# The four sums of each attention head's features, made by GpSimd instead of VectorE

## The chip, the cores and the metric

One Trainium2 chip, one core. The metric is the time of the whole kernel on the device in microseconds, as the median of repeated executions. TensorE (PE) multiplies, VectorE (DVE), ScalarE (ACT) and GpSimd (POOL) do elementwise work, SyncE (SP) issues transfers; POOL issues transfers as well. Each engine works through its own instructions in the order in which they stand in the program. Engines wait for each other through semaphores.

## The reference

32 graphs of 512 nodes. Each goes through a layer norm with ReLU and two graph attention layers (four heads of 256 features, then one head of 512), and the result is added to the input. Cut to what matters here:

```python
def gat_layer(x, mask, W, a_src, a_dst, bias, concat):
    xl = (x @ W).reshape(B, N, H, F)
    asrc = jnp.einsum('bnhf,hf->bnh', xl, a_src)
    adst = jnp.einsum('bnhf,hf->bnh', xl, a_dst)
    e = jax.nn.leaky_relu(asrc[:, :, None, :] + adst[:, None, :, :], 0.2)
    e = jnp.where(mask[..., None], e, -1e9)
    attn = jax.nn.softmax(e, axis=1)
    out = jnp.einsum('bsdh,bshf->bdhf', attn, xl)      # the gather
    ...
h = jnp.maximum(_layernorm(x, axis=-1), 0.0)
h = jax.nn.elu(gat_layer(h, mask, W1, att_src1, att_dst1, b1, concat=True))
x = x + gat_layer(h, mask, W2, att_src2, att_dst2, b2, concat=False)
```

All of it is f32.

## The kernel before

**Products by seven.** The large products are made by a scheme of the Strassen kind: each operand is cut into two by two blocks, sums and differences of blocks are formed, and seven block products take the place of eight. The first gather, attention times features of one head, is one of them. `sums1` (L1277) forms the sums for one head: on the left from the features `xl` (s1 = a21 + a22, s2 = s1 - a11, a21 = a11 - a21, s4 = a12 - s2; 128 x 256 elements each), on the right from the attention `p` (t1, t2 and two more; 128 x 512 each). s1, s2 and s4 are put into `hs`, the third one is written over a block of `xl`. s4 takes the place of s2 and so can only be made when the sixth product has read s2; the third product needs it. For the last graph (`apart`) s4 has a place of its own, `hs4`. `gather1` (L1334) runs the seven products of the heads, two heads at a time (`PAIRS_OF`): 1, 5, 2, 6, 7, 3, 4, each for one head and then for the other. One product is a step of two matmuls on PE, into one of eight PSUM banks (`mm`). Behind it ACT or DVE takes the result out (`h1` in names of the trace is `h`), or, after the first product, ACT copies the bank into a second one in which the second product goes on adding (`mm<-mm`). The bank is free for others after that.

The first gather is made in this way for 31 of the 32 graphs; graph 0 uses plain products (`gather1_plain`). That makes 31 x 4 heads with four sums of features each.

**What runs beside it.** The loop over graphs (L1611) interleaves the first gather of one graph with the projection of the next one (`project1`: `ht` times `w1_sb` (`w_sb` in the trace), with sums of its own in `hs`, `hx` and `wx`, into `xl`), the projection to the second layer (`project2`: `h1` times `w2_sb`, into `xl2`) and the second gather (`gather2`). The attention `p` of a head is made in `second` (L948): DVE adds and takes the maximum, POOL issues two transfers that add the mask to `p` in place (`p<-dm`, `accumulate`, L522), ACT takes the exponential. Then DVE makes the sums of `p`. POOL has besides these transfers one small operation a graph, the power in the norm (L770).

**What sets the order.** The code doesn't issue its work where it stands. `Program.add` records every step with its engine, a cost written out by hand, and what it reads and writes. At the end `order` (L299) runs a list scheduler over all of it: each engine takes, of the steps whose inputs are there by the costs and by a table of latencies between engines (`PAIRS`, `CROSS`), the one with the lowest rank. A rank is a due time out of the long table `PLACES`, repeated for each graph. The transfers of SP and POOL run on modelled queues. The steps are then issued in the order that comes out, and on the chip each engine keeps to it, whether the costs were right or not. So the cost and the engine of a step have a say in the order of all the others. The table of ranks is the same before and after.

Of the kernel before, what the change touches and what calls it, by code (L numbers as in the profile page):

```python
# [378 lines left out]
def tile_gat(  # L379
# [36 lines left out]
    nc = tc.nc  # L416
# [94 lines left out]
    prog = Program()  # L511
# [3 lines left out]

    def dve(cost, reads, writes, f, *a, **k):
        prog.add("DVE", cost, reads, writes, lambda: f(*a, **k))  # L517

    def dma(size, reads, writes, to, at, cost=0.4):
        prog.add("SP", cost, reads, writes, lambda: nc.sync.dma_start(to, at), size)  # L520
# [46 lines left out]
    def sums_of_weights(w_sb, keys, cost):  # L567
        b11, b21, b22, t4, t1, t2, t3 = (w_sb[:, i] for i in range(7))
        sub = nc.vector.tensor_sub
        dve(cost, keys(6) + keys(0), keys(4), sub, t1, t3, b11)  # L570
        dve(cost, keys(2) + keys(4), keys(5), sub, t2, b22, t1)
        dve(cost, keys(2) + keys(6), keys(6), sub, t3, b22, t3)
        dve(cost, keys(1) + keys(5), keys(3), sub, t4, b21, t2)
# [253 lines left out]
    def p_keys(pk, us=range(NT), cs=range(2)):  # L827

        return [pk + (u, c) for u in us for c in cs]
# [447 lines left out]
    def sums1(h, pk, p, apart):  # L1277


        def a_block(i, j):  # L1280
            return (
                xl[:, 2 * j : 2 * j + 2, h, 2 + i * P : 2 + (i + 1) * P],
                [("xl", 2 * j + k, h, i) for k in range(2)],
            )

        def b_block(r, c):
            return (
                p[:, 2 * r : 2 * r + 2, c * M : (c + 1) * M], p_keys(pk, (2 * r, 2 * r + 1), (c,))
            )

        a11, a12, a21, a22 = (a_block(i, j) for i in range(2) for j in range(2))
        b11, b12, b21, b22 = (b_block(r, c) for r in range(2) for c in range(2))
        k = KQ + h % 2
        s1, s2 = (
            (hs[:, i, k, :].rearrange("p (k f) -> p k f", f=P), [("hs", i, k)]) for i in range(2)
        )
        s4 = s2
        if apart:
            s4 = (hs4[:, h % 2, :].rearrange("p (k f) -> p k f", f=P), [("hs", 2, h % 2)])
        t1, t2 = (  # L1300
            (t.rearrange("p (k f) -> p k f", f=M), [q]) for q, t in (ts_.take() for _ in range(2))
        )

        def op(cost, f, to, u, v):
            dve(cost, u[1] + v[1], to[1], f, to[0], u[0], v[0])

        add, sub = nc.vector.tensor_add, nc.vector.tensor_sub
        op(0.34, add, s1, a21, a22)
        op(0.602, sub, t1, b12, b11)
        op(0.34, sub, s2, s1, a11)  # L1310
        op(0.602, sub, t2, b22, t1)
        op(0.34, sub, a21, a11, a21)
        op(0.602, sub, b12, b22, b12)
        if apart:
            op(0.34, sub, s4, a12, s2)
        return (
            {1: a11, 2: a12, 3: s4, 4: a22, 5: s1, 6: s2, 7: a21},
            {1: b11, 2: b21, 3: b22, 4: b21, 5: t1, 6: t2, 7: b12},
            lambda: op(0.602, sub, b21, b21, t2),
            (lambda: None) if apart else (lambda: op(0.34, sub, s4, a12, s2)),  # L1320
        )


# [10 lines left out]
    def gather1(soft, order):  # L1334
# [3 lines left out]
        for h in sorted(ahead):  # L1338
            blocks[h] = sums1(h, *soft.p[h], order is SINGLY)
        for h, n in order:  # L1340
            if h not in blocks:
                blocks[h] = sums1(h, *soft.p[h], order is SINGLY)
# [367 lines left out]
```

## Time and profile before

| what | us |
|---|---|
| median of the runs shown (2766.06 and 2766.17) | 2766.11 |
| span of the profiled execution | 2767.6 |
| granted TensorE clock, mean | 0.999 of full |
| ACT busy | 2229.1 |
| POOL busy with issuing mask transfers (314) | 273.2 |
| DMA engines, mean busy share from 100 to 2600 us | 0.69 |

The span runs from the first to the last instruction of the program in one profiled execution; the median is that of executions timed by themselves. Names: `out<-in` are the program's tiles. L517 records all of DVE's steps, L514 ACT's, L531 PE's, so groups are told apart by tiles. A PE step of two matmuls stands in the trace as four instructions. In the rows of a group stand the busy time, the mean of one in ns, and then the idle time of the engine just before, with what ended it. A row of the timeline has the start, the duration, the engine, and in brackets the idle time before it. A row of waits has the total, the number and the longest.

### The profile page before, as it was taken

To read this page: it belongs to the slowest core of one execution; us is meant where nothing else is said; L and a number is where in the kernel's file an instruction comes from. 1 tells how busy PE (TensorE), PEld (TensorE's weight loads), DVE (VectorE), ACT (ScalarE), POOL (GpSimd) and SP (SyncE) were. 2 spreads that over 40 slices of the span, in tenths; PEclk is the share of its full clock that TensorE was granted. 3 is DMA by queue.
4 is the path that set the end of the run, shared out by engine and by line. 5 is a ranking of instruction groups with operands and counts; after the bars stand their busy time and mean duration, and the time that the engine had idled before them with its cause. 6 is when DMAs were issued, how large, how long until landed. Compare 5 with 4: busy or idle time off the path is not lost. (4 is left out here: it accounts for less than half of the span.)

```text
span 2767.6 us, 42320 instructions
## 1 busy us (share of the span) xinstructions
PE 2742.4 (99%) x12924; PEld 2371.8 (86%) x12924; DVE 2558.2 (92%) x6732; ACT 2229.1 (81%) x4907; POOL 313.1 (11%) x356
## 2 busy tenths in 40 slices
PE   7999999999999999999999999999999999999999
PEld 6788888888888888888888888888888888888887
DVE  8999999999999999999999999999999999999996
ACT  5978888778887788877888877888778788788883
POOL 0110111101111111111011111111111111101110
PEclk9999999999999999999999999999999999999999
DMA  8657766667666667667676766766676767767563
GB/s 232 176 157 182 203 167 184 187 176 194 182 183 179 182 176 196 178 175 195 173 201 172 182 187 178 192 186 180 180 188 175 201 167 180 195 165 208 162 171 112
DMA packets 375864, 502.14 MB, mean 181 GB/s; under 512 B 222804, under 2 KB 227668, under 8 KB 375636
## 3 DMA queue, kind: packets, MB, share of 16 engines
q1 hardware_dynamic: 329844, 332.68, 42.4%
q0 software_dynamic: 45792, 166.74, 25.1%
q8 instruction: 103, 1.69, 0.3%
q14 instruction: 125, 1.02, 0.1%
HBM read 316.41 MB, written 51.31 MB: 133 GB/s over the span
## 5 line engine op out<-in xcount | busy, mean ns | idle before, releaser
L531 PE MATMUL mm<-w_sb,hs 128*128 128x257 f32 (+3 forms) x2908 | 667.0, 367 | 5.1 <-ACT mm L514 3.3
L531 PEld LDWEIGHTS mm<-w_sb,hs 128*128 128x128 f32 x2908 | 539.7, 190 | 87.7 <-ACT mm L514 6.7
L525 POOL DMA_DIRECT2D p<-dm x314 | 273.2, 875 | 2295.0 <-DVE p L517 764.3
L531 PE MATMUL mm<-w_sb,ht 128*128 128x258 f32 x2112 | 528.6, 382 | 2.7 <-ACT mm L514 2.5
L531 PE MATMUL mm<-p,xl 128*128 128x258 f32 (+1 forms) x1984 | 495.8, 383 | 0.1
L531 PE MATMUL mm<-w_sb,h 128*128 128x257 f32 x2056 | 477.8, 379 | 0.0
L517 DVE SCALAR_TENSOR_TENSOR p<-rr,z 128x512 f32<-128x512 f32 (+1 forms) x636 | 456.0, 742 | 2.4 <-DMA rr<-drr 2.4
L531 PEld LDWEIGHTS mm<-w_sb,ht 128*128 128x128 f32 x2112 | 393.7, 190 | 63.6 <-ACT mm L514 6.4
L514 ACT ACTIVATE p<-p,z 128x512 f32<-128x512 f32 (+1 forms) x636 | 433.4, 720 | 17.7 <-DVE p L517 12.4
L531 PEld LDWEIGHTS mm<-w_sb,h 128*128 128x128 f32 x2056 | 389.0, 189 | 58.4 <-ACT xl L514 0.5
L531 PEld LDWEIGHTS mm<-p,xl 128*128 128x128 f32 x1984 | 367.2, 190 | 52.7 <-issue 6.0
L514 ACT ACTIVATE mm<-mm 128x257 f32<-128x257 f32 (+2 forms) x498 | 169.8, 347 | 269.2 <-PE mm L531 236.2
L514 ACT ACTIVATE l<-as,z 128x512 f32<-128x512 f32 x516 | 354.4, 716 | 30.8 <-DMA as<-das 30.7
L514 ACT ACTIVATE l<-l,low 128x512 f32<-128x512 f32 x516 | 370.3, 721 | 7.6 <-DVE low L517 6.7
L517 DVE CUSTOM_DVE_ANT_1 l<-l,mt 128x512 f32<-128x512 f32 x516 | 346.2, 681 | 28.4 <-ACT l L514 27.4
L514 ACT ACTIVATE xl<-mm 128x258 f32<-128x258 f32 (+2 forms) x748 | 269.3, 382 | 91.4 <-PE mm L531 89.8
L514 ACT ACTIVATE h<-mm,b_sb 128x256 f32<-128x256 f32 (+1 forms) x504 | 231.0, 480 | 77.3 <-PE mm L531 76.6
L531 PE MATMUL mm<-t,hs 128*128 128x258 f32 (+1 forms) x992 | 246.1, 380 | 0.0
L517 DVE TENSOR_TENSOR xl<-xl,mm 128x258 f32<-128x258 f32 x372 | 155.3, 419 | 57.9 <-PE mm L531 48.3
L531 PEld LDWEIGHTS mm<-t,hs 128*128 128x128 f32 x992 | 185.8, 190 | 25.5 <-DVE t L517 0.2
L531 PE MATMUL mm<-xl,p 128*128 128x258 f32 (+2 forms) x752 | 189.7, 388 | 1.0 <-ACT h L514 0.6
L517 DVE SCALAR_TENSOR_TENSOR h<-xr,h 128x512 f32<-128x512 f32 x256 | 172.2, 683 | 6.1 <-ACT xr L514 6.1
(137 smaller groups left out, 3706.2 us busy)
## 6 DMA issues: line engine op xcount, KB each, us to landing
p<-dm POOLq DMA_DIRECT2D x314, 512.0 KB, 5.0
rr<-drr SPq DMA_DIRECT2D x159, 512.0 KB
x<-in_x_dram SPq DMA_DIRECT2D x129, 256.0 KB
adj<-in_adj_dram SPq DMA_DIRECT2D x128, 256.0 KB
as<-das SPq DMA_DIRECT2D x64, 512.0 KB
t<-in_x_dram SPq DMA_DIRECT2D x124, 256.0 KB
out_dram<-t SPq DMA_DIRECT2D x124, 256.0 KB
dm<-m SPq DMA_DIRECT2D x64, 256.0 KB
```

Source lines behind the costliest of these rows:

```text
L514: prog.add("ACT", cost, reads, writes, lambda: nc.scalar.activation(*a, **k))
L517: prog.add("DVE", cost, reads, writes, lambda: f(*a, **k))
L525: lambda: nc.gpsimd.dma_start(to, at, accum_op=OP.add), size,
L531: f(*a, **k)
```

## The change

A helper `pool` records steps for POOL, and the four sums of features in `sums1` are recorded through it, with a cost of 0.75 in place of 0.34. The sums of `p` stay on DVE. What is computed is the same.

```diff
+    def pool(cost, reads, writes, f, *a, **k):
+        prog.add("POOL", cost, reads, writes, lambda: f(*a, **k))
+
...
-        add, sub = nc.vector.tensor_add, nc.vector.tensor_sub
-        op(0.34, add, s1, a21, a22)
+        def feature(f, to, u, v):
+            pool(0.75, u[1] + v[1], to[1], f, to[0], u[0], v[0])
+
+        sub = nc.vector.tensor_sub
+        feature(nc.gpsimd.tensor_add, s1, a21, a22)
         op(0.602, sub, t1, b12, b11)
-        op(0.34, sub, s2, s1, a11)
+        feature(nc.gpsimd.tensor_sub, s2, s1, a11)
         op(0.602, sub, t2, b22, t1)
-        op(0.34, sub, a21, a11, a21)
+        feature(nc.gpsimd.tensor_sub, a21, a11, a21)
         op(0.602, sub, b12, b22, b12)
         if apart:
-            op(0.34, sub, s4, a12, s2)
+            feature(nc.gpsimd.tensor_sub, s4, a12, s2)
...
-            (lambda: None) if apart else (lambda: op(0.34, sub, s4, a12, s2)),
+            (lambda: None) if apart else (lambda: feature(nc.gpsimd.tensor_sub, s4, a12, s2)),
```

The lines of the changed kernel are numbered three higher from here on (L534 is PE's). The order of the steps changes on every engine. Three places:

PE, where the fourth product of one head (into bank `mm_136`, from `p_103`) is followed by the first of the next pair (`p_102`, into the same bank), amid steps of the projection (operands `w_sb`, `ht`, `hs`, `hx`, `wx`). Before:

```order
L531 MATMUL mm_136<-p_103,xl 128x256 x2
L531 MATMUL mm_138<-w_sb,hs 128x129
L531 MATMUL mm_137<-wx_85,hx_86 128x129
L531 MATMUL mm_132<-w_sb,ht 128x258 x2
L531 MATMUL mm_137<-w_sb,hs 128x129
L531 MATMUL mm_138<-w_sb,hx_86 128x129
L531 MATMUL mm_136<-p_102,xl 128x258
L531 MATMUL mm_136<-p_102,xl 128x256
L531 MATMUL mm_137<-wx_85,hs 128x129
L531 MATMUL mm_138<-w_sb,hs_84 128x258 x2
L531 MATMUL mm_137<-w_sb,ht 128x258 x2
```

The same place now:

```order
L534 MATMUL mm_132<-w_sb,ht 128x258 x2
L534 MATMUL mm_133<-p_104,xl 128x256 x2
L534 MATMUL mm_139<-w_sb,ht 128x258 x2
L534 MATMUL mm_136<-p_103,xl 128x256 x2
L534 MATMUL mm_136<-p_102,xl 128x258
L534 MATMUL mm_136<-p_102,xl 128x256
L534 MATMUL mm_133<-p_102,xl 128x256 x2
L534 MATMUL mm_132<-w_sb,hs 128x258 x2
```

The first product of the new head now stands directly behind the fourth of the old one, whose bank ACT has to empty in between, and directly behind it stands its second product (`mm_133`), for which ACT has to copy the bank first; before, five rows of the projection stood at the first of these places and five, three of which are shown, at the second.

PE, in the projection of the same graph, with bank `mm_133`. Before:

```order
L531 MATMUL mm_133<-w_sb,hs 128x258 x2
L531 MATMUL mm_135<-w_sb,hs 128x258 x2
L531 MATMUL mm_133<-w_sb,ht 128x258 x2
L531 MATMUL mm_139<-w_sb,hs_84 128x258 x2
L531 MATMUL mm_135<-w_sb,ht 128x258 x2
```

Now:

```order
L534 MATMUL mm_139<-w_sb,hs_84 128x258 x2
L534 MATMUL mm_133<-w_sb,hs 128x258 x2
L534 MATMUL mm_133<-w_sb,ht 128x258 x2
L534 MATMUL mm_135<-w_sb,ht 128x258 x2
L534 MATMUL mm_137<-w_sb,hs_84 128x258 x2
```

The step of `mm_135` that stood between the two steps of `mm_133` has moved away.

POOL, over some half of a graph, with the mask transfers (DMA) of a few heads. Before:

```order
L525 DMA p_103<-dm_122 128x1024 x2
L525 DMA p_104<-dm_121 128x1024 x2
L525 DMA p_102<-dm_121 128x1024 x2
L770 TENSOR_TENSOR stats_123<-stats_123,half 128x4
L525 DMA p_103<-dm_121 128x1024 x2
```

Now:

```order
L528 DMA p_102<-dm_121 128x1024
L520 TENSOR_TENSOR hs<-xl 128x256 x2
L520 TENSOR_TENSOR xl<-xl 128x2x128 x2
L528 DMA p_102<-dm_121 128x1024
L773 TENSOR_TENSOR stats_123<-stats_123,half 128x4
L520 TENSOR_TENSOR hs<-hs,xl 128x256 x2
L520 TENSOR_TENSOR hs<-xl 128x256
L520 TENSOR_TENSOR xl<-xl 128x2x128
L520 TENSOR_TENSOR hs<-xl 128x256
L520 TENSOR_TENSOR xl<-xl 128x2x128
L520 TENSOR_TENSOR hs<-xl,hs 128x256
L528 DMA p_103<-dm_121 128x1024 x2
```

Four sums now stand between the two mask transfers of one head (`p_102`), and seven sums and the power ahead of those of the next (`p_103`).

## The prediction

> **What bounds the kernel now.** I read the page's busy times first, then what TensorE (PE) waited for, then the groups of VectorE (DVE) and GpSimd (POOL), then single places of the timeline.
>
> ```profile
> span 2767.6 us, 42320 instructions
> PE 2742.4 (99%) x12924; PEld 2371.8 (86%) x12924; DVE 2558.2 (92%) x6732; ACT 2229.1 (81%) x4907; POOL 313.1 (11%) x356
> ...
> PE mm L531 <- ACT x L514: 12.1, 1, 12.1
> PE mm L531 <- ACT mm L514: 5.8, 10, 1.2
> PE mm L531 <- DVE hs L517: 1.3, 1, 1.3
> ```
>
> PE is busy for 2742.4 of 2767.6 us, so it is the bound, and only 25.2 us are left to win, 0.9%. Of these, 12.1 us are one wait at the start. In the steady part PE waits for ScalarE (ACT) ten times, 5.8 us together. DVE has 2767.6 - 2558.2 = 209 us of idle time, POOL is idle for 89% of the span. So work taken off DVE is taken off an engine that does not set the end. What can change the time is whether PE still finds its operands ready.
>
> The profiled execution's span is 2767.6 us, 1.5 us above the median of the runs shown (2766.11). I make the sum on the span and take 1.5 off at the end. Two per cent of 2766 is 55.3 us, about what a measurement of this kernel tells from no change; "slower" below means over 2821.4 us.
>
> **The change part by part.** 31 graphs x 4 heads x 4 sums are 496 operations. They leave DVE:
>
> ```profile
> L517 DVE TENSOR_TENSOR hs<-xl,hs 128x256 f32<-128x256 f32 x124 | 52.0, 419 | 4.4 <-PE mm L531 4.1
> L517 DVE TENSOR_TENSOR hs<-hs,xl 128x256 f32<-128x256 f32 x124 | 51.7, 419 | 0.0
> L517 DVE TENSOR_TENSOR hs<-xl 128x256 f32<-128x256 f32 x124 | 50.5, 420 | 0.9 <-PE mm L531 0.9
> L517 DVE TENSOR_TENSOR xl<-xl 128x256 f32<-128x256 f32 x124 | 49.5, 418 | 0.0
> ...
> 717.17 0.75 DVE L517 TENSOR_TENSOR hs<-xl 128x256 f32<-128x256 f32 x2
> ```
>
> Two in a row take 0.75 us where one takes 0.42, so each holds up the next by 0.33 to 0.34 us: DVE is relieved of 496 x 0.336 = 167 us. By itself that is worth nothing, since DVE has idle time already.
>
> *Price of one sum on POOL.* No row shows it. The nearest ones:
>
> ```profile
> L770 POOL TENSOR_TENSOR stats<-stats,half 128x4 f32<-128x4 f32 x32 | 35.9, 1120 | 97.9 <-DVE stats L517 96.2 <-ACT l L514 1.7
> masks.py:199 POOL TENSOR_SCALAR_AFFINE_SELECT identf<-identf 128x128 f32<-128x128 f32 x1 | 0.3, 292 | 0.1
> masks.py:197 POOL MEMSET identf<- 128x128 f32 x1 | 0.2, 204 | 0.3 <-POOLq L1696 0.3
> ...
> L1696 POOL MEMSET const-float32-0.0<- 128x1 f32 x1 | 0.1, 98 | 0.2 <-issue 0.2
> ```
>
> One element costs 98 ns, so 0.10 us is fixed. A write costs (204 - 98)/127 = 0.83 ns an element, a read and a write (292 - 98)/127 = 1.53 ns, so a read adds 0.70 ns. With one read, 256 elements take 0.10 + 0.39 = 0.49 us, the low end. With two reads, 0.10 + 256 x 2.23 ns = 0.67 us. The high end lets the power of the norm (1.12 us for four elements, waits included) stand for the fixed part: 1.12 + 0.57 = 1.7 us. I take 0.67, as the select is the nearest kind of work. [...]
>
> *The new order, the largest term.* The costs of all steps enter the planner, so PE's order is another one too, as the two places on PE in the part on the change show. Its rows say which bank a step writes, and the code says who empties it. I followed every step of both orders by what it reads and writes, and counted the PE steps that need a result which ACT or DVE makes out of an earlier PE step with hardly any PE work between. Directly behind the step it depends on: 3 before, 74 now (58 through ACT, 16 through DVE). With one 129-column matmul between: 3 before, 28 now. With two such narrow ones between, 0.45 us: 2 before, 32 now. What such a place costs is shown at those that before has:
>
> ```profile
> 45.82 0.60 PE L531 MATMUL mm<-w_sb,ht 128*128 128x258 f32 x2
> 46.94 0.48 PE L531 MATMUL mm<-w_sb,ht 128*128 128x258 f32 x1 [0.53 <-ACT mm L514]
> ...
> 46.52 0.37 ACT L514 ACTIVATE mm<-mm 128x258 f32<-128x258 f32 x1
> ...
> 2689.54 0.48 PE L531 MATMUL mm<-xl,p 128*128 128x258 f32 x1 [0.57 <-ACT h L514]
> ...
> 54.44 0.38 PE L531 MATMUL mm<-w_sb,hs 128*128 128x129 f32 x1 [0.46 <-DVE mm L517]
> ...
> 794.22 1.89 PE L531 MATMUL mm<-xl,hs 128*128 128x256 f32 x8
> 795.94 1.90 PE L531 MATMUL mm<-w_sb,h 128*128 128x257 f32 x8
> ```
>
> PE ends at 46.42, ACT starts 0.10 us later, runs 0.37, and PE goes on 0.05 us after that: 0.53 us empty, and 0.57 and 0.46 at the two others. I take 0.55. A full matmul takes (795.94 - 794.22)/4 = 0.43 us (two traced instructions each), a narrow one half, 0.22. So 74 x 0.55 + 28 x (0.55 - 0.22) + 32 x (0.55 - 0.45) = 40.7 + 9.2 + 3.2 = 53.1 us; the same count for before gives 2.8. The order costs **+50 us**. Low end 74 x 0.46 = 34; high end 134 x 0.57 = 76, if whatever left PE without other work also comes late. No wait of before's ten can hide it: these are chains from PE to PE.
>
> *The wait of POOL against DVE.* The only two-input operation that POOL has now shows what it meets:
>
> ```profile
> 717.41 1.07 POOL L770 TENSOR_TENSOR stats<-stats,half 128x4 f32<-128x4 f32 x1 [1.42 <-DVE stats L517]
> ...
> 95.78 1.22 DVE L517 TENSOR_TENSOR w_sb<-w_sb 128x1028 f32<-128x1028 f32 x1
> ...
> 95.59 2.28 POOL L770 TENSOR_TENSOR stats<-stats,half 128x4 f32<-128x4 f32 x1
> ...
> 201.08 0.74 DVE L517 SCALAR_TENSOR_TENSOR p<-rr,z 128x512 f32<-128x512 f32 x1
> ...
> 201.32 1.40 POOL L770 TENSOR_TENSOR stats<-stats,half 128x4 f32<-128x4 f32 x1 [29.17 <-DVE stats L517]
> ```
>
> POOL ends 0.87 us after DVE's sum of weights (97.87 against 97.00), 0.90 after the product (202.72 against 201.82) and 0.89 after the first of the two feature sums at 717 (718.48 against 717.59), however long it had run by then. So POOL stands still until a DVE operation with two SBUF inputs has ended. [...]
>
> ```profile
> L517 DVE SCALAR_TENSOR_TENSOR p<-rr,z 128x512 f32<-128x512 f32 x628 | 452.5, 746 | 1.2 <-DMA rr<-drr 1.2
> L517 DVE CUSTOM_DVE_ANT_1 l<-l,mt 128x512 f32<-128x512 f32 x516 | 346.2, 681 | 28.4 <-ACT l L514 27.4
> L517 DVE SCALAR_TENSOR_TENSOR h<-xr,h 128x512 f32<-128x512 f32 x256 | 172.2, 683 | 6.1 <-ACT xr L514 6.1
> ```
>
> These three are 971 us of two SBUF inputs; with the sums over p, h and ht it is about 60% of the span. If DVE stands still in its turn, it loses between nothing and 496 x 0.67 = 332 us. With a two-input operation next in about half of the cases I get 0.35 us each, 174 us, which eats up the 167 won. DVE is then as loaded as before, but late by a third of a microsecond at 16 places a graph. Of that, PE sees the part that finds no slack: low end 0, high end all 174. Before, PE waited directly for DVE little over 2 us in all, so I stay near the low end: **+25 us**, a seventh.
>
> *The fourth sum.* It sits between a head's sixth and third product, as it writes where the sixth has read. In the new order at least 1.5 us of PE work lies there in 120 of 124 cases, in most of them two full steps or more, 4 x 0.43 = 1.7 us. [...] Hidden, except at four places with one step (0.86): **+2 us**. At 1.7 us for a sum that cover is gone at some 50 places more, by half a microsecond each, 25 us.
>
> *POOL's queue.* The mask transfers are issued there, 314 before and after; the order puts up to eleven sums between two pairs.
>
> ```profile
> p<-dm POOLq DMA_DIRECT2D x314, 512.0 KB, 5.0
> ...
> ACT p L514 <- DMA p<-dm: 5.2, 8, 1.4
> ```
>
> ACT waited for them 5.2 us in eight cases, so they land in time now. A sum that waits on a PE step holds up the transfers behind it. Between 0 and 30 us; **+5 us**. SP's transfers are the same ones, in another order: nothing, as PE's waits name no SP transfer.
>
> *Sum.* 2767.6 + 50 + 25 + 2 + 5 = 2849.6, less 1.5: **2848 us**.
>
> **The rivals.**
>
> *Not slower.* POOL's sums find room, DVE is really relieved by 167 us, and only the order costs: 2767.6 + 50 - 1.5 = 2816 us, within 2%. For it speaks DVE's idle time and POOL's 89%; against it, that 5 us more than the order's 50 already pass the limit. It decides at 0.55 us a place: with ACT's answer in 0.4 us this ends at about 2798. If the new order cost nothing, 2766. Chance 0.25 together. Faster by over 2% would need 55 us where PE has 25 to give: 0.01.
>
> *DVE becomes the bound.* [...] Chance 0.10. [...]
>
> *The masks come late.* If every second one of the 157 pairs waits for one sum of 0.67 plus 0.35 us and nothing hides it, 2816 + 79 = 2895 us, with ACT's exponentials waiting for p. Chance 0.07.
>
> **How the numbers follow.** My forecast, between 2822 and 2885, has 0.57; with 0.10 and 0.07 for the last two rivals, slower has 0.74, same 0.25, faster 0.01. The range goes down to 2808 (the order's term at its lower half, the rest hidden) and up to 2915, with about one in ten left out on each side.
>
> **What would show it.** After: PE's busy time still near 2742 us, its idle time 85 to 130 us, and most of that behind ACT mm, xl and h, in some 75 to 130 waits of half a microsecond. POOL's sums last 0.67 us where DVE runs one-input work and up to 0.7 more where not. DVE's two-input operations beside a POOL sum are longer, or start late. If PE's waits behind ACT stay near 6 us, the order term is wrong. [...] If a sum lasts over 1.2 us, the fourth sums show as waits of PE for POOL. A wait of ACT for the mask transfers far over 5 us shows the last rival.

## The result, and the profile after

The changed kernel takes 3126.6 us (median; 3121.2 to 3132.1) against 2766.1 us: 1.129 of before, with a 95% interval of 1.127 to 1.131. Forecast were 2848 us, and at most 2915. The direction was right, the size was off by a factor of more than four: 360 us lost where 82 were forecast.

The page of the changed kernel begins so (busy time, share of the span, instructions):

```profile
span 3119.3 us, 42781 instructions
PE 2863.5 (92%) x12924; PEld 2388.0 (77%) x12924; DVE 2622.0 (84%) x6236; ACT 2264.7 (73%) x4907; POOL 759.2 (24%) x852
```

DVE has 496 instructions fewer and is nevertheless busy for longer than before (2558.2). PE, which had 1% of its span free, now has 8%. TensorE's waits in the changed kernel (total, number, longest):

```profile
PE mm L534 <- ACT mm L514: 39.6, 49, 2.5
PE mm L534 <- issue: 29.1, 18, 2.9
PE mm L534 <- DVE h L517: 29.0, 25, 3.4
PE mm L534 <- DVE p L517: 23.6, 24, 3.8
PE mm L534 <- ACT h L514: 19.6, 15, 2.7
PE mm L534 <- DVE mm L517: 16.9, 18, 3.2
PE mm L534 <- DVE hs L517: 15.8, 14, 2.2
PE mm L534 <- POOL hs L520: 15.5, 23, 1.7
```

No single wait was added: PE waits for everything a little, and GpSimd's sums are a small part of it. Of PE's waits of over 0.15 us there were 17 before, 21.0 us together, and 12 of them were shorter than 0.7 us (4.8 us). Now there are 241, 246.9 us together: 136 shorter than 0.7 us with 52.8 us, and 105 longer ones with 194.1 us. Nearly all of the rest of the 352 us that the span grew by is in PE's busy time, 121 us more for the same matmuls; the last section says of what.

The groups of DVE and POOL in the changed kernel that answer to those quoted ahead:

```profile
L517 DVE SCALAR_TENSOR_TENSOR p<-rr,z 128x512 f32<-128x512 f32 x628 | 506.6, 842 | 1.8 <-DMA rr<-drr 1.8
L517 DVE CUSTOM_DVE_ANT_1 l<-l,mt 128x512 f32<-128x512 f32 x516 | 360.5, 716 | 68.8 <-ACT l L514 67.8
...
L520 POOL TENSOR_TENSOR xl<-xl 128x256 f32<-128x256 f32 x124 | 124.0, 1035 | 3.7
L520 POOL TENSOR_TENSOR hs<-xl 128x256 f32<-128x256 f32 x124 | 123.9, 1014 | 157.6 <-PE mm L534 140.5 <-ACT mm L514 11.9 <-ACT adj L514 3.8
L520 POOL TENSOR_TENSOR hs<-xl,hs 128x256 f32<-128x256 f32 x124 | 110.9, 897 | 595.3 <-PE mm L534 595.2
L520 POOL TENSOR_TENSOR hs<-hs,xl 128x256 f32<-128x256 f32 x124 | 98.3, 804 | 126.6 <-PE mm L534 123.9 <-DVE x L517 2.2
```

A sum is recorded with 0.94 us in the mean of the four groups, and DVE's product `p<-rr,z`, which is not part of the change, went from 746 to 842 ns.

### The profile page after: what moved, and what is told of

It is laid out like the page before. It is cut to its first block, busy times and chain, and to the rows that moved or that the text cites. A ratio compares the mean times of both kernels' runs of the same rounds, so it can differ in the third digit from the quotient of the medians.

```text
span 3119.3 us, 42781 instructions
## 1 busy us (share of the span) xinstructions
PE 2863.5 (92%) x12924; PEld 2388.0 (77%) x12924; DVE 2622.0 (84%) x6236; ACT 2264.7 (73%) x4907; POOL 759.2 (24%) x852
## 5 line engine op out<-in xcount | busy, mean ns | idle before, releaser
L534 PE MATMUL mm<-w_sb,hs 128*128 128x257 f32 (+3 forms) x2908 | 681.9, 372 | 48.3 <-DVE hs L517 14.7
L534 PEld LDWEIGHTS mm<-w_sb,hs 128*128 128x128 f32 x2908 | 542.8, 191 | 142.8 <-DVE mm L517 18.9
L534 PE MATMUL mm<-p,xl 128*128 128x258 f32 (+1 forms) x1984 | 525.9, 397 | 59.9 <-DVE p L517 23.6
L534 PE MATMUL mm<-w_sb,ht 128*128 128x258 f32 x2112 | 537.7, 388 | 44.0 <-DVE h L517 18.0
L517 DVE SCALAR_TENSOR_TENSOR p<-rr,z 128x512 f32<-128x512 f32 (+1 forms) x636 | 510.1, 838 | 5.4 <-DMA rr<-drr 5.4
L534 PEld LDWEIGHTS mm<-w_sb,ht 128*128 128x128 f32 x2112 | 391.5, 191 | 128.1 <-DVE h L517 24.5
L534 PE MATMUL mm<-w_sb,h 128*128 128x257 f32 x2056 | 480.9, 380 | 8.0 <-DVE xl L517 4.4
L534 PEld LDWEIGHTS mm<-p,xl 128*128 128x128 f32 x1984 | 371.3, 194 | 145.3 <-DVE p L517 32.9
L534 PEld LDWEIGHTS mm<-w_sb,h 128*128 128x128 f32 x2056 | 388.4, 189 | 69.4 <-DVE xl L517 6.4
L514 ACT ACTIVATE xl<-mm 128x258 f32<-128x258 f32 (+2 forms) x748 | 277.3, 378 | 204.7 <-PE mm L534 201.5
L517 DVE CUSTOM_DVE_ANT_1 l<-l,mt 128x512 f32<-128x512 f32 x516 | 360.5, 716 | 68.8 <-ACT l L514 67.8
L534 PE MATMUL mm<-t,hs 128*128 128x258 f32 (+1 forms) x992 | 264.1, 394 | 55.2 <-issue 27.6
L534 PEld LDWEIGHTS mm<-t,hs 128*128 128x128 f32 x992 | 189.6, 197 | 98.2 <-issue 40.4
L520 POOL TENSOR_TENSOR hs<-xl,hs 128x256 f32<-128x256 f32 x124 | 110.9, 897 | 595.3 <-PE mm L534 595.2
```

Of the source, the lines that this page charges most:

```text
L514: prog.add("ACT", cost, reads, writes, lambda: nc.scalar.activation(*a, **k))
L520: prog.add("POOL", cost, reads, writes, lambda: f(*a, **k))
```

## The experiments

The change does two things at once: it moves the sums to another engine, and through the planner it gives all engines another order. The experiments take the two apart. Kernels of "the order of X" have the same rows in the same order on TensorE; what is swapped is only the engine that executes the four sums. Where the sums are left out, GpSimd fills their blocks with a constant. A fill is shorter than a sum (338 to 421 ns in the mean of a group in e3 and e4, against 0.94 us in the changed kernel) and doesn't wait for the sum's inputs, so a step from fills to sums holds all that a sum on GpSimd costs over a fill, not the blocking of VectorE alone.

| us (median) | sums on VectorE | fills on GpSimd | sums on GpSimd |
|---|---|---|---|
| order of before | 2766.1 | 2767.6 (e4) | 2863.4 (e2) |
| order of the changed kernel | 3061.7 (e1) | 2989.3 (e3) | 3126.6 |
| order by due times | 2896.8 (e11) | 2840.2 (e12) | 3012.7 (e9) |

e3 and e4 are one run each, the others two to ten. Before was timed again beside each batch, at 2767 to 2769 us in the median.

**e1: the new order, the sums on VectorE.**

```diff
-            pool(0.75, u[1] + v[1], to[1], f, to[0], u[0], v[0])
+            g = nc.vector.tensor_add if f == nc.gpsimd.tensor_add else nc.vector.tensor_sub
+            pool(0.75, u[1] + v[1], to[1], g, to[0], u[0], v[0])
```

(`pool` only tells the planner; `g` is what is issued.)

> The order of the changed kernel on every engine, but the four sums are executed by VectorE, at the place that the planner gave them. Theory 'order' (the steps stand in a worse order, and that is the loss): about 3100 us. Theory 'lock' (a sum on GpSimd and a two-input operation of VectorE stand in each other's way, and that is the loss): about 2820 us, which is before plus the 50 us that the prediction gave the order. Theory 'latency' (a sum on GpSimd just takes longer than planned, 0.94 us with its waits instead of 0.75): also about 2820 us. VectorE busy near 2558 us again, its mean product p<-rr,z near 746 ns.

3061.7 us, ratio 1.106 (1.104 to 1.107). No sum is on GpSimd, `p<-rr,z` is back at 748 ns, and most of the loss is there. The theory "order" holds, and my 50 us for it don't. (e1 also keeps on VectorE the sums that this order counts on being elsewhere; e3 takes them away.)

**e2: the old order, the sums on GpSimd.**

```diff
-            pool(0.75, u[1] + v[1], to[1], f, to[0], u[0], v[0])
+            dve(0.34, u[1] + v[1], to[1], f, to[0], u[0], v[0])
```

> The four sums are executed by GpSimd, but every step keeps the order that it had before the change (the planner still takes them for VectorE's, at 0.34). Theory 'lock': over 3000 us, with VectorE's two-input operations lengthened as in the changed kernel (p<-rr,z at about 840 ns). Theory 'order': under 2800 us. Theory 'latency': over 2900 us too, as the fourth sum sits in a window of 0.9 to 1.7 us between two products, but with VectorE's operations at their old times.

2863.4 us, ratio 1.034 (1.032 to 1.035): outside what all three theories had said. In the old order the sums on GpSimd cost 96 us, less than the order does in e1. In e2's groups the product is longer still, as "lock" had it, but PE's waits name GpSimd, as "latency" would have it; e6 and e7 tell these two apart:

```profile
L517 DVE SCALAR_TENSOR_TENSOR p<-rr,z 128x512 f32<-128x512 f32 x628 | 520.0, 860 | 2.3 <-DMA rr<-drr 2.0
...
PE mm L534 <- POOL hs L517: 57.4, 56, 3.0
```

**e3 and e4: fills on GpSimd, in the new and in the old order.** The four sums are left out in both.

```diff
-            pool(0.75, u[1] + v[1], to[1], f, to[0], u[0], v[0])
+            pool(0.75, u[1] + v[1], to[1], nc.gpsimd.memset, to[0], 0.5)
```

(e4 with `dve(0.34, ...)`, as in e2.)

> The order of the changed kernel; in the place of each of the four sums GpSimd fills the same block with a constant, which reads nothing (so the sums are left out). About 0.31 us each by the two fills that the profile before shows. Theory 'lock' (what reads on GpSimd blocks VectorE): VectorE's operations back at their old times (p<-rr,z near 746 ns), near 2820 us. Theory 'order': about 3100 us with VectorE's times old. If writing alone also blocks VectorE: p<-rr,z between 746 and 840 ns and a time in between.

> The order of before, and GpSimd fills the blocks in place of the four sums (left out). Both theories: near 2770 us, since neither the order nor a read on GpSimd is there; 'latency' gives the same, as a fill is about as short as VectorE's sum. If it is over 2850 us, what hurts is the mere crossing to GpSimd and back, or writes there.

e3 takes 2989.3 us, e4 2767.6. A group of DVE and one of POOL, first of e3, then of e4:

```profile
L517 DVE SCALAR_TENSOR_TENSOR p<-rr,z 128x512 f32<-128x512 f32 x628 | 445.9, 747 | 1.9 <-DMA rr<-drr 1.8
...
L520 POOL MEMSET hs<- 128x256 f32 x372 | 121.1, 338 | 1007.4 <-PE mm L534 993.8 <-issue 8.8 <-DVE stats L517 1.0
```

```profile
L517 DVE SCALAR_TENSOR_TENSOR p<-rr,z 128x512 f32<-128x512 f32 x628 | 450.2, 747 | 26.2 <-issue 24.0 <-DMA rr<-drr 2.2
...
L517 POOL MEMSET hs<- 128x256 f32 x372 | 126.5, 350 | 786.4 <-PE mm L534 755.7 <-DVE low L517 27.4
```

A fill reads nothing and doesn't lengthen the product: 747 ns against 746 before. So writing these blocks on GpSimd doesn't hold the product, and the sums, which read two blocks, do (842 ns in the changed kernel, 860 in e2); an operation that reads one was not tried. Nor does taking the blocks from GpSimd cost anything by itself: in e4 PE waited for them once, for 0.3 us. e4 says one more thing: with the sums off VectorE, a short fill in their place and the old order, the time is that of before. In this order there was nothing to win.

Read along the table's middle column, the new order costs 2989.3 - 2767.6 = 222 us. Read along its second row, sums on GpSimd instead of fills cost 3126.6 - 2989.3 = 137 us, and 96 us in the old order. So the order is the larger part.

**e5: a cost of 0.339 instead of 0.34, nothing else.** Is it the move that spoils the order?

```diff
-        op(0.34, add, s1, a21, a22)
+        op(0.339, add, s1, a21, a22)
```

(so for all four)

> The kernel before, with the cost of the four sums written as 0.339 instead of 0.34; they stay on VectorE, and no instruction changes its engine or size. Theory 'any change of a cost spoils the order, since the table of ranks fits one set of costs only': over 2950 us, with waits of TensorE like those of the changed kernel. Theory 'moving the sums to another engine, with its longer cost, spoils the order': within 0.5% of 2766 us.

3070.9 us, ratio 1.109 (1.108 to 1.111). No instruction has changed its engine or size. PE's order departs from the old one with a single swap, after some 170 of 3350 rows. The order of e5 against that of before:

```
 L531 MATMUL mm_133<-w_sb,ht 128x258 x2
+L531 MATMUL mm_139<-x_88,hs 128x258
+L531 MATMUL mm_139<-x_88,hs 128x257
 L531 MATMUL mm_137<-xl_80,p_102 128x258
 L531 MATMUL mm_137<-xl_80,p_102 128x257
-L531 MATMUL mm_139<-x_88,hs 128x258
-L531 MATMUL mm_139<-x_88,hs 128x257
```

From there on it never finds back: PE's rows of e5 and of before have 2214 lines of difference, those of the changed kernel and of before 2315. Its waits are of the same kind:

```profile
PE mm L531 <- ACT mm L514: 52.0, 55, 2.1
PE mm L531 <- ACT h L514: 26.1, 25, 4.0
PE mm L531 <- DVE hs L517: 21.5, 16, 4.3
```

So an edit of 0.3% in one cost spoils the order about as the move did. None of the edits of this cost that were tried with the table of ranks (0.339 here, 0.75, and 0.77 in e8) kept the time: the kernels are 8 to 13% slower, the last two with the sums on GpSimd.

**e6 and e7: the old order, three sums or only the fourth on GpSimd.**

```diff
-            feature(nc.gpsimd.tensor_sub, s4, a12, s2)
+            feature(nc.vector.tensor_sub, s4, a12, s2)
```

(e6; e7 the other way round, s1, s2 and a21 on `nc.vector`; `feature` as in e2)

> The order of before; three of the four sums (s1, s2, a21) are executed by GpSimd, the fourth (s4) by VectorE. Against 2863 us with all four on GpSimd and 2766 with none. If what costs there is the fourth sum in its short window: about 2785 us, TensorE's 57 us of waits for GpSimd's hs nearly gone, though VectorE still loses some 0.5 us to each of the 372 sums (195 us more in its operations). If what costs is VectorE's blocking: about 2840 us, three quarters of the loss.

> The order of before; only the fourth sum (s4) is executed by GpSimd, the other three by VectorE. If the window of the fourth sum is what costs: 2830 to 2850 us, with 50 to 60 us of waits of TensorE for GpSimd's hs. If VectorE's blocking is what costs: about 2790 us, a quarter of the loss.

e6: 2847.4 us, ratio 1.029 (1.027 to 1.030). e7: 2790.5 us, 1.008 (1.006 to 1.009). Against before in the same batch that is 80 us for three sums and 23 for one: it goes roughly by the number of sums, not by the window of the fourth. PE's waits in e6 show how the blocking reaches PE. They don't name GpSimd once; the fourth sum is VectorE's again, and is late because VectorE is:

```profile
PE mm L534 <- DVE hs L517: 31.6, 31, 1.3
...
310.64 1.06 POOL L517 TENSOR_TENSOR xl<-xl 128x256 f32<-128x256 f32 x1
...
309.90 1.21 DVE L517 TENSOR_TENSOR t<-p,t 128x512 f32<-128x512 f32 x1
311.04 1.21 DVE L517 SCALAR_TENSOR_TENSOR p<-rr,z 128x512 f32<-128x512 f32 x1
312.17 0.41 DVE L517 TENSOR_TENSOR hs<-xl,hs 128x256 f32<-128x256 f32 x1
...
312.69 0.45 PE L534 MATMUL mm<-p,hs 128*128 128x256 f32 x1 [0.64 <-issue]
```

The two operations ahead of the fourth sum (`hs<-xl,hs`) take 1.21 us each beside GpSimd's sums, where before they took 0.68 and 0.75, and PE stands empty until 0.1 us after it. The view puts this wait down to "issue", but it ends behind the same sum: 54 waits of e6, 46 us, end so, 27 of them named "issue".

**e8: a cost of 0.77 instead of 0.75 in the changed kernel.**

```diff
-            pool(0.75, u[1] + v[1], to[1], f, to[0], u[0], v[0])
+            pool(0.77, u[1] + v[1], to[1], f, to[0], u[0], v[0])
```

> The changed kernel with the cost of the four sums written as 0.77 instead of 0.75: the same instructions on the same engines, in another order. Theory 'order': clearly another time than 3127 us, by 50 us or more, and I expect 3000 to 3050. Theory 'GpSimd and VectorE block each other, whatever the order': 3127 us within 1%.

2999.4 us: 127 us less than the changed kernel with the same instructions on the same engines.

**e9 and e10: ranks that are due times.** The planner runs once with the costs of before, and the start times that it gives are the ranks of the second run, which makes the order.

```diff
     def emit(self):
+        jobs = self.jobs
+        self.jobs = [self.was.get(j, q[:2]) + q[2:] for j, q in enumerate(jobs)]
+        self.order()
+        self.jobs, self.due = jobs, self.start
         for j in self.order():
             self.jobs[j][3]()
```

(`was` holds engine and cost before the change, and `ranks` returns `due`. e9 is the changed kernel, e10 is e5.)

> The changed kernel (four sums on GpSimd, planned at 0.75 there), but the planner's ranks are not the table's: they are the start times that the planner gave each step before the change. TensorE's order then differs from that of before in 284 rows instead of 2315. Theory 'the table fits one set of costs only': 2800 to 2880 us, about what the same sums cost in the order of before (2863). Theory 'the cost of 0.75 on another engine forces a bad order': still over 3000 us.

> The kernel before with the cost 0.339 instead of 0.34, as in e5, and the ranks made of the planner's start times, as in e9. TensorE's rows are those of before, so 2766 us within 0.5% if the order on TensorE with what follows from it is all that e5 lost; over 2900 us if something else in e5 was at fault, as the orders of the transfers or of VectorE.

e10 is back at 2767.0 us, ratio 1.000 (0.999 to 1.001): with due times the 0.339 does no harm, so what e5 lost was the order. e9 takes 3012.7 us (1.086 to 1.091), though PE's order is nearly the old one. That is the number of the second theory and not of the first; but the second had spoken of the order alone, and e12 below gives that 73 us. Both had left out the other engines, whose orders differ more (some 3000 lines of difference on DVE, against 284 on PE; the "rows" of the expectations are such lines).

**e11 and e12: the order of e9, with the sums on VectorE, and with fills.** The edits are those of e1 and e3, on e9:

```diff
             prog.was[len(prog.jobs)] = ("DVE", 0.34)
-            pool(0.75, u[1] + v[1], to[1], f, to[0], u[0], v[0])
+            pool(0.75, u[1] + v[1], to[1], nc.gpsimd.memset, to[0], 0.5)
```

(e12, which leaves the four sums out; e11 with `g` of e1 in place of `f`)

> The order of e9 on every engine, but the four sums are executed by VectorE. If e9 loses its 9% by the order (TensorE's 284 rows, or VectorE's, which differs in some 3000): 2950 to 3015 us. If it loses it because GpSimd and VectorE block each other in a plan that counts on a relieved VectorE: under 2850 us.

> The order of e9; in place of the four sums GpSimd fills the blocks (sums left out), at some 0.34 us each and without blocking VectorE. If the order loses: over 2900 us. If the blocking loses: 2770 to 2830 us, and the difference to e9 is what blocking costs in this order, against 96 us in the order of before.

e11: 2896.8 us (1.045 to 1.049). e12: 2840.2 us (1.024 to 1.027). No expectation of either is met, e12 missing that of "blocking" by 10 us: the order alone, 73 us with fills, loses less than e9 does, but more than "blocking" had allowed. Sums instead of fills cost 3012.7 - 2840.2 = 172 us in this order, against 137 and 96 in the others. VectorE's operations are longer by about as much as elsewhere (199 us in e9, 204 in the changed kernel, 215 in e2), so more of it reaches PE here. That this is so because the order counts on a free VectorE is a reading that no run tests.

## Why the prediction was wrong

**What bounds the kernel: right.** PE was the bound, with 0.9% to win; e4 shows that in the old order even sums that cost VectorE nothing win nothing.

**The price of a sum: right.** 0.67 us was taken. In the changed kernel 18 sums ran while VectorE did nothing, from 0.63 us on and 0.67 in the mean. That the sum made of a fill and a select came out so exactly is in part luck. The 0.94 us of all sums hold more: waiting for VectorE, and, where sums stand behind each other, the tail of the one before (in the last section's timeline four sums are over in 3.13 us, but each is recorded with 1.05 to 1.08).

**"The order costs +50 us": the step that failed.** The order cost 222 us where +50 was taken. What I counted, places where PE stands directly behind its own result, gives short waits, and there the size is right only by luck: waits under 0.7 us went from 4.8 to 52.8 us, +48, but 18 of them, 8.1 us, are for GpSimd's sums, which weren't in the count, and in e3, with the same rows on PE and the product `p<-rr,z` at 747 ns, they are 33.9 us, +30 over e4. The error was to take that count for the whole term. Its high end (76 us) allowed only for the counted places being later. Of the 222 us the longer waits make 110 (125.3 in e3, 15.2 in e4), and PE's busy time 78. A long wait can arise where a step that PE needs stands behind others that are late themselves, which no pair of PE rows shows. One such, from the timeline of the changed kernel (start, duration, operation; in brackets the idle time before):

```profile
1014.17 0.69 DVE L517 SCALAR_TENSOR_TENSOR h<-xr,h 128x512 f32<-128x512 f32 x1 [1.42 <-ACT xr L514]
1014.78 0.69 DVE L517 BATCH_NORM_STATS2 stats<-x 128x6 f32<-128x512 f32 x1
1015.38 0.68 DVE L517 TENSOR_TENSOR t<-p 128x512 f32<-128x512 f32 x1
1015.97 0.69 DVE L517 CUSTOM_DVE_ANT_1 l<-as,mt 128x512 f32<-128x512 f32 x1
1016.58 0.08 DVE L517 DVE_READ_ACCUMULATOR2_ANT low<- 128x1 f32 x1
1016.58 1.41 DVE L517 SCALAR_TENSOR_TENSOR p<-rr,z 128x512 f32<-128x512 f32 x2
1017.91 0.30 DVE L517 TENSOR_TENSOR mm<-mm,f 128x129 f32<-128x129 f32 x1
...
1018.26 0.65 PE L534 MATMUL mm<-w_sb,hs 128*128 128x129 f32 x2 [3.00 <-DVE mm L517]
```

PE stands empty for 3.00 us behind a sum of 0.30 us. That sum waits for nothing but its place: VectorE starts it after a chain of longer steps that began 1.42 us late. How many of the 105 long waits are of this kind was not followed up; in e3 the long ones that name an engine are mostly for ACT. With the sums still on VectorE the same order costs 296 us (e1).

**"VectorE late by 174 us, PE sees 25": half of it failed.** No run shows either number; that VectorE is held at all was my assumption, and both were estimates on it. By the groups, VectorE's operations became 204 us longer in the changed kernel and 215 in e2 (number times the difference of the means to before, summed), 0.41 and 0.43 us a sum where 0.35 was taken. That was close. What failed is the seventh that was to reach PE: in the old order about a half did (e6: operations longer by 158 us, the kernel by 80; e2: 215 and 96, the fourth sum's own lateness included), and in the new one 137 us. I argued from PE's rare direct waits for VectorE before, but those were rare because VectorE was on time.

**The fourth sum and POOL's queue.** No run shows the +2 us, which was my estimate, and it was too little: in e7, which moves it alone and costs 23 us, PE's waits for GpSimd are 10.7 us, in 29 waits. The masks were right: ACT waited 8.4 us for them, in 7 waits, after 5.2.

**The rivals.** "Not slower" fell by far. "DVE becomes the bound" is not what happened either: VectorE is idle for 497 of 3119 us, and still late in many places. No engine is busy throughout in the changed kernel (PE, the busiest, for 92%): the engines wait for each other in turn.

## What to carry to other kernels

Where a planner with a table fitted to its costs sets the order, an edit of one cost is a new kernel: test it first as e5 does, with the cost changed and nothing moved, and judge a move in the old order (e2). Counting close pairs of rows in an order leaves out its long waits: here it gave 50 us of 222. And before taking work off an engine, fill the blocks in place of computing them (e4): if that wins nothing, don't expect a win from moving the work in that order.

## What the runs showed of the hardware

**GpSimd can hold VectorE over several instructions.** From the changed kernel's timeline:

```profile
592.96 3.77 DVE L517 SCALAR_TENSOR_TENSOR p<-rr,z 128x512 f32<-128x512 f32 x1
...
593.05 1.75 POOL L520 TENSOR_TENSOR hs<-xl 128x256 f32<-128x256 f32 x2
594.44 1.74 POOL L520 TENSOR_TENSOR xl<-xl 128x256 f32<-128x256 f32 x2
```

A product of 0.75 us lasts 3.77, as long as four sums on GpSimd stand behind each other: VectorE does not get its turn between them. I had expected turns, one sum at most (0.67 us). It is rare: of the 628 products of the changed kernel two met four sums, and lasted 3.77 and 3.83 us; 62 others met two, and none of these lasted over 1.30. The fills of e3 and e4, which read nothing, left the product at 747 ns in the mean.

The prediction took two SBUF inputs of a VectorE operation for the condition, and the case shows more than that. `h<-h,mm`, whose second input lies in a PSUM bank, keeps its time (415 ns before, 413 in the changed kernel, 409 in e2), in accord with it; but `z<-z` of 128x4, a small operation with one input, goes from 132 ns to 692 in the mean of 32, and is at 470 in e2 against 156 with the fills of e4.

**Half clock after half-empty stretches.** In the changed kernel the granted TensorE clock falls to 0.5 at 22 places, nearly always for 3.41 us or a multiple of it, 103 us together, against 6 us at two places before. Three such stretches in a row (length, busy times and counts, clock):

```profile
1015.04:1018.45 3.41, 0.41 (x3) 0.21 (x3) 3.41 (x8) 0.86 (x3) 0.00 (x0) 1.00 0.02 5
1018.45:1021.86 3.41, 3.41 (x12) 2.95 (x12) 3.26 (x8) 1.07 (x4) 0.89 (x1) 0.50 0.50 121
1021.86:1025.28 3.42, 3.42 (x18) 2.98 (x17) 2.44 (x9) 0.74 (x3) 0.87 (x1) 1.00 0.57 126
```

The wait of 3.00 us above is followed by 3.41 us at half clock. PE need not have been empty all the time: ahead of each fall it had been idle for 1.79 us or more of the 3.41 us before. That is no sure sign: from 1677.2 to 1680.6 us PE was busy for 1.43 us only, and the clock stayed at 1.00. But a long wait can be paid for once more. PE was busy for 85 of the 103 us, and by an estimate from the clock of 0.5 half of that is lost, 43 us against 2 before: some 41 of the 121 us by which PE's busy time grew. Most of the rest fits the 224 additional waits: the first matmul after one lasts 0.484 us where others last 0.379 and doesn't overlap the one before by 0.163, so 0.27 us each, by an estimate 60 us; this was not tried by itself.
